# A hybrid of scan, attention and STU on one core: a convolution half in thirds, first products ahead of the scans, longer attention tails, tables of the last STU fetched earlier

## The chip, the core and the metric

The kernel runs on one core of a Trainium2 chip. The metric is the device time of one execution in microseconds, the median of several. The engines are TensorE (PE, its weight loads PEld), VectorE (DVE), ScalarE (ACT), GpSimd (POOL) and SyncE (SP), which here issues nearly all DMAs. Each engine works through its own instruction list in order; semaphores tie them together.

## The reference, cut to what matters

Input x has shape (4, 48, 48, 128), so 4 images of L = 2304 tokens with 128 channels, all in float32.

```python
# layer 0
xz = x_groupnormed @ in_proj_w.T             # 2 * 256 channels: xin, z
xc = silu(depthwise_conv3x3(xin) + conv_b)   # 256 channels = two halves of 128
xs = four orders of xc (rows, columns, both reversed)
dt = softplus(dt_proj(x_proj(xs)))
h  = h * exp(dt * A) + dt * xs * B           # 4 scans, 16 states, 2304 steps
y  = sum of the scans, layernorm, * silu(z)
x  = x + y @ out_proj_w.T
# layer 1
t  = x + softmax(n(x) n(x)^T) n(x)           # n: layernorm over channels
t  = t + STU(n(t))                           # 16 causal convolutions along the tokens, each projected
```

## The kernel before, in words

**Stages.** The images go through a pipeline of stages, one after the other in time. The opening (`prologue`) normalises an image, projects it and computes the convolution. The scans of an image run over 24 chunks (4 orders, 6 chunks of 384 tokens), each with 8 units of 4 scans. Then an epilogue and the attention of that image follow; the next image's `prologue` and the first steps of its scans are woven into the attention. The STU of an image runs on TensorE beside the scans of the next image; beside image 0's scans a mixture of weights is computed instead. The last image's STU (`stu3`) has no scans to run beside, and comes alone at the end.

**Opening.** `taps(h)` computes the 3x3 convolution of channel half h on VectorE, by 9 instructions over the whole image (128x2304): one at L276, eight at L278. `silu(h)` follows in three thirds: tanh on ScalarE (L287), the product on VectorE (L291). The padded input `xpad` stands in a pool called `turn`. For image 0, `run` issues all of the prologue, then `begun` runs through `begin_scans`, whose steps prepare the first chunks: a projection of `xc` on TensorE (L412), copied to `xd` (L419); a second projection (L429) copied to `dt` (L432); softplus (L443); `dx` = dt times xc (L465); both stored to DRAM (L454) and loaded back replicated over partitions as `rep` (L459); rows of `xd` are loaded as `bc` (L485). `start_y` then sets up the sums `ya` (L325). Chunks in row order take 8 image rows each.

**Scans.** A `Ring` of 4 or 5 buffers in PSUM holds the decays. Its constructor zeroes two columns of each buffer on VectorE (L341). `scans` first spreads two `bc` rows into ring buffers (L500), enters two units (L508, on VectorE, or on POOL for three of the eight) and computes decays with exp (L517). Then, for each unit, it issues four scans (L524), and between them `more(share)` takes so many steps of the generator `work` (STU or mixture) as the share of its columns asks. The first step of `conv` in the STU uses tables `tt`, of which the first are loaded in the attention; ScalarE copies results between its products (L1208, L1212, L1215, L1216), issued some columns late (`later`, `do_late`).

**Attention.** `attention` runs over five pieces of queries with 18 key tiles each: 90 slots. A slot issues a product s (L852), its exp (L854), and the value product of three slots before (L844). When a piece is done, its `tail` advances by one step in each slot: the sum is copied from PSUM (oT, L1043), transposed on TensorE (otr, L1047), divided by its denominator and added to T (L1050 to L1058), stored (L1060), loaded back in another token order (L1066), normalised (statistics L1072 to L1078, the result u on ScalarE at L1082), half sums taken (L1084), transposed (utr, L1088), copied and stored. For the last image a tail ends after L1060. In each slot pieces of the next prologue, sorted by cost, are woven in.

**The last STU.** `stu3` loads for each item (block, filter) five tables (L1422) and a weight tile G (L1425), two items ahead; at a block's start inputs `ux`, the mixed weights `mue` and the residual (L1431 to L1436). Per item there are five products (L1446), copies and sums, and a projection (L1480) one item later. `finish3` prepares the inputs of later blocks beside it; its load `fx` is L1361, its statistics L1365.

What sets the order: the lists are written out by the generators above, in program order, with no planner. All DMAs of one engine's queue are issued in order, and a DMA first waits until an earlier one on its semaphore, eight issues back, has landed.

Of the kernel before, what the change touches and what calls it, by code (L numbers as in the profile page):

```python
# [8 lines left out]
F32 = mybir.dt.float32  # L9
# [51 lines left out]
def hybrid_kernel(ctx: ExitStack, tc: tile.TileContext, a: dict, out: bass.AP):  # L61
# [118 lines left out]
    def prologue(b, pool, mm_tile):  # L180
# [87 lines left out]
        def nothing():  # L268
            pass

        def taps(h):
            def tap(t):
                dy, dx = divmod(t, 3)
                x = xpad[:, dy:dy + H, dx:dx + W]
                if t == 0:
                    nc.vector.tensor_scalar(xc[h], x, cw[:, h, 0:1], cb[:, h:h + 1], ALU.mult, ALU.add)  # L276
                else:
                    nc.vector.scalar_tensor_tensor(xc[h], x, cw[:, h, t:t + 1], xc[h], ALU.mult, ALU.add)  # L278
            return [(nothing, Slow(lambda t=t: tap(t), 2.65), t == 0) for t in range(9)]

        def silu(h):
# [30 lines left out]
        for i in range(n):  # L312
            proj(1, i, 0)
            if i % 2:
                tasks.append(zs_[9 + i // 2])
                tasks.append(silu(0)[i // 2])
        tasks.extend(taps(1))
        tasks.extend(silu(1))
        return tasks

    def start_y(b):

# [12 lines left out]
    class Ring:  # L335


        def __init__(self, pool, n, name):
            self.t = [pool.tile([P, 512], F32, tag=f"ring{i}", name=f"{name}_{i}") for i in range(n)]
            for t in self.t:  # L340
                nc.vector.memset(t[:, 0:CS + 2:CS + 1], 0.0)  # L341
            self.free = list(range(n))

        def take(self):
# [263 lines left out]
    def scans(b, chunks, preps, front, sp, back, ring, finish, work, work_cols):  # L608

        units = [Unit(ch, h, q) for ch in chunks for h, q in quads]  # L610
        total = len(chunks) * CHUNK_COLS + work_cols
        done = [0]

        def more(share):

            while done[0] < share * total:
                cols = next(work, None)
                if cols is None:
                    break
                done[0] += cols  # L620

        def enter(s):

            if s + 2 < len(units) and units[s + 2].pool:
                units[s + 2].enter(sp.s, ring)
            if 0 <= s + 1 < len(units) and not units[s + 1].pool:
                units[s + 1].enter(sp.s, ring)

        wanted, issued = [], [0]

        def fill(left=0):

            while wanted and ring.free:
                wanted.pop(0).spread(ring)
            while len(ring.free) > left and issued[0] < G4 * len(units):
                i = issued[0]
                issued[0] += 1
                units[i // G4].decay(i % G4, ring)

        def scan(s, g):  # L640
            fill()
            units[s].scan(g, ring)

        def spread(s):
            if s < len(units) and not units[s].pool:
                wanted.append(units[s])

        def prepare(s):

            ci, j = divmod(s, len(quads))  # L650
            for c in range(ci + 1, ci + 5):
                if c < len(chunks) and 0 <= s - len(quads) * c + LEAD[c % 2] < STEPS[c % 2]:
                    done[0] += next(preps[c]) or 0

        def refill(s, i):

            if 0 <= s < len(units) and s // len(quads) + 1 < len(chunks):
                u, nxt = units[s], chunks[s // len(quads) + 1]
                if u.h == NH - 1:
                    nxt.fetch(i + u.q, front)  # L660

        pending = []
        spread(0)
        fill(len(ring.free) - 1)
        enter(-2)
        enter(-1)
        spread(1)
        fill(1)
        for s in range(len(units) + 2):
            real = s < len(units)  # L670
            enter(s)
            prepare(s)
            if real:
                scan(s, 0)
            more((s + 0.25) / len(units))
            next(finish, None)
            if 1 <= s <= len(units):
                units[s - 1].times_c(s >= len(units) - (units[0].ch.b == 0))
            if real:
                scan(s, 1)  # L680
            if pending:
                pending.pop().add_y()
            prepare(s)
            more((s + 0.5) / len(units))
            next(finish, None)
            spread(s + 2)
            if real:
                scan(s, 2)
            more((s + 0.75) / len(units))
            next(finish, None)  # L690
            prepare(s)
            if real:
                scan(s, 3)
            refill(s - 2, Q4)
            refill(s + 1, 0)
            if s >= 2:
                units[s - 2].sum_c(back.psy)
                done[0] += CS
                if units[s - 2].q == Q4 - 1:
                    pending.append(units[s - 2])  # L700
            more((s + 1) / len(units))
            next(finish, None)
        for u in pending:
            u.add_y()
        for _ in work:
            pass
# [330 lines left out]
    def tail(b, J, T, po, pool, ps, last):  # L1037
# [4 lines left out]
        oT = pool.two.tile([P, 512], F32, tag="oT", name=f"oT{b}_{J}")  # L1042
        nc.vector.tensor_copy(oT[:, :P * n], po[:, :P * n])  # L1043
        yield
        p = ps.trs.tile([P, 4, C], F32, tag="tr", name=f"otr{b}_{J}")[:, :n]
        for j in range(n):
            nc.tensor.transpose(p[:, j], oT[:, j * P:(j + 1) * P], ident)  # L1047
# [34 lines left out]
            nc.scalar.activation(u[:k, J, j], x[:k, j], AF.Identity, bias=mv[:k, j, 3:4], scale=mv[:k, j, 2:3])  # L1082
        yield
        nc.vector.tensor_tensor(sums[:k, J], u[:k, J, 0:2], u[:k, J, 2:4], ALU.add)  # L1084
        yield
        p = ps.trs.tile([P, 512], F32, tag="tr", name=f"utr{b}_{J}")[:, :4 * k]
        for j in range(4):
# [305 lines left out]
            yield  # L1393
        nc.sync.dma_start(ud3[:, :, 1 + P * G:1 + P * (G + 1)], x)

    def stu3(b, pool, ps, u3, ue):

# [7 lines left out]
        tts, Gs, S, U, now = {}, {}, {}, {}, {}  # L1407
        last = pool.one.tile([P, KF], F32, tag="last", name="last3")
        nc.vector.memset(last, 0.0)
        PT = (3, 1, 4, 0, 2)  # L1410
        Y = 3 * (P + 1)

        def fetch(n):
            if n >= len(items):
                return
            bl, k = items[n]
            hi = P * (bl + 1)
            for pt in PT:
                t = tts[n, pt] = pool.tt.tile([P, 2 * L3], F32, tag="tt", name=f"t3{n}_{pt}")[:, :2 * hi].rearrange(
                    "p (e i) -> p e i", e=2)  # L1420
                row = fd3[k, pt, 0]
                nc.sync.dma_start(t, bass.AP(row.tensor, row.offset + L3 - hi, [[1, P], [L3 + P, 2], [1, hi]]))  # L1422
            parts = PARTS3[bl]
            Gs[n] = pool.tt3.tile([P, 2, 3, C], F32, tag="G", name=f"G3{n}")
            nc.sync.dma_start(Gs[n][:, :, :len(parts)], gd[k, :, :, parts[0][2]:parts[-1][2] + 1])  # L1425

        def begin(bl):
            parts = PARTS3[bl]
            lo, hi = P * bl, P * (bl + 1)
            now["x"] = pool.one.tile([P, 8, P], F32, tag="ux", name=f"ux3{bl}")  # L1430
            nc.sync.dma_start(now["x"][:, 2:], ud3[:, :, 1 + lo:1 + hi])  # L1431
            nc.sync.dma_start(now["x"][:, :2], ud3[:, 4:, lo:hi])
            now["mu"] = pool.one.tile([P, 3, 3, C], F32, tag="mue", name=f"mue3{bl}")
            nc.sync.dma_start(now["mu"][:, :len(parts)], mud[:, parts[0][2]:parts[-1][2] + 1])
            now["T", bl] = pool.two.tile([P, 6, C], F32, tag="res", name=f"res3{bl}")
            nc.sync.dma_start(now["T", bl], td[6 * lo:6 * hi].rearrange("(p j) c -> p j c", j=6))  # L1436

# [122 lines left out]
        for _ in other:  # L1560
            pass

    def begun(pieces):

        for x in pieces:
            pass
        return x

    def stu_alone(b, env):
        work = stu(b, env, 1)  # L1570
        next(work)
# [5 lines left out]
        pool.close()  # L1577
        tabs.close()

    turn = Stage(tc, "p", "left", one=(1, SB))  # L1580
    begin0 = Stage(tc, "pp", "right", mm=(4, PSUM))
    once = Stage(tc, "once", "right", one=(1, SB))
    bank["mm"] = begin0.mm, ("t",)
    run(prologue(0, turn.one, mm_tile), 3, weights(once.one))
    turn.close()
    once.close()
    front = Stage(tc, "f0", "left", one=(1, SB), xd=(2, SB), rep=(3, SB))
    first = begun(begin_scans(0, front))
    begin0.close()
    start_y(0)  # L1590
    for b in range(B):
# [13 lines left out]
        turn = Stage(tc, f"t{b}", "left", one=(1, SB))  # L1605
        if b + 1 < B:
            tabs = Stage(tc, f"k{b}", "right", four=(4, SB))
        back = Stage(tc, f"a{b}", "right", one=(1, SB), two=(2, SB), five=(5, SB))
        xn = back.one.tile([P, NT, C], F32, tag="xn", name=f"xn{b}")
        xnT = back.one.tile([P, L], F32, tag="xnT", name=f"xnT{b}")  # L1610
# [31 lines left out]
        for i in range(slots - BEGIN):  # L1642
            next(at)
            if not more:
                next(made, None)
            while parts and (spent < share * (i + 1) or i == slots - BEGIN - 1):
                spent += costs.pop(0)
                parts.pop(0)()
        if more:
            turn.close()  # L1650
            front = Stage(tc, f"f{b + 1}", "left", one=(1, SB), xd=(2, SB), rep=(3, SB))
# [17 lines left out]
    ps = Stage(tc, "endp", "right", psa=(1, PSUM), psc=(2, PSUM), psi=(1, PSUM), psp=(1, PSUM))  # L1669
    bank["mm"] = ps.psa, ("mm",)  # L1670
    ended = (x for G in range(1, N3) for x in finish3(G, extra, u3, ue))
    for i, _ in enumerate(stu3(B - 1, pool, ps, u3, ue)):
        next(ended, None)
    ps.close()
    pool.close()
    extra.close()


# [57 lines left out]
```

## Time and profile before

| | us |
|---|---|
| median of 3 runs | 5449.74 |
| lowest, highest | 5448.53, 5450.31 |
| the profiled execution | 5450.86 |
| its span in the profile | 5448.9 |
| PE busy | 4753.7 (87%) |
| DVE busy | 4320.4 (79%) |
| ACT busy | 3213.1 (59%) |
| POOL busy | 3646.6 (67%) |

Roughly, in the span: opening of image 0 until 117, its scans until 1060, epilogue and attention until 1299; then scans and STU from 1299 to 2260, 2497 to 3460 and 3690 to 4660, with attentions between; the last STU from 4843 on. Shares over the whole span mix these stages, so each stage has to be read by itself. A timeline line gives the start, the busy time, the engine, the source line, the operation with its output and inputs, its shape and its number; in brackets stands the idle time of the engine ahead of it, and what ended it. `SPq` are DMA issues.

### The profile page before, as it was taken

How to read it: one execution, taken by the hardware profiler on the slowest of the kernel's cores; microseconds unless marked ns; L12 is line 12 of the kernel's file. 1: busy time of each engine (PE TensorE's matmuls, PEld its weight loads, DVE VectorE, ACT ScalarE, POOL GpSimd, SP SyncE). 2: the span in 40 equal slices, each digit the busy share in tenths (PEclk: the TensorE clock that was granted, in tenths of full speed). 3: DMA queues.
4: the chain of work that ended last, by engine and by line, in shares of the span. 5: the costliest groups of instructions: out<-in, count | busy, mean ns of one | idle time of the engine just before them, and what ended most of it. 6: DMA issues, size and time to landing. Idle time of an engine off the chain costs nothing. (4 is left out here: it accounts for less than half of the span.)

```text
span 5448.9 us, 71245 instructions
## 1 busy us (share of the span) xinstructions
PE 4753.7 (87%) x23372; PEld 3059.5 (56%) x23372; DVE 4320.4 (79%) x5308; ACT 3213.1 (59%) x6829; POOL 3646.6 (67%) x1881
## 2 busy tenths in 40 slices
PE   4656655698999999998999999898999999989999
PEld 1211211255666666645666666545666666559987
DVE  7999999856999999856999999658999999423211
ACT  3666666546777767456777766457777666432111
POOL 1999998713989999605999999407999999201100
PEclk7777777799999999999999999999999999999999
DMA  4445545404887777416777787227877786136543
GB/s 123 157 156 171 171 153 165 128 27 143 248 257 254 251 258 253 134 34 193 239 259 254 242 269 252 84 75 208 252 246 260 249 262 230 37 83 153 151 142 91
DMA packets 732184, 996.11 MB, mean 183 GB/s; under 512 B 108968, under 2 KB 580648, under 8 KB 731752
## 3 DMA queue, kind: packets, MB, share of 16 engines
q1 hardware_dynamic: 725992, 988.26, 57.6%
q10 hardware_dynamic: 5824, 3.30, 0.3%
q8 instruction: 187, 3.06, 0.2%
q14 instruction: 181, 1.48, 0.1%
HBM read 873.03 MB, written 118.31 MB: 182 GB/s over the span
## 5 line engine op out<-in xcount | busy, mean ns | idle before, releaser
L524 DVE TENSOR_TENSOR_SCAN s<-ring,s 128x385 f32<-128x385 f32 x3072 | 2691.5, 935 | 88.8 <-ACT ring L517 88.0
L534 POOL TENSOR_TENSOR s<-s,bc 128x1536 f32<-128x1536 f32 x763 | 2423.4, 3179 | 95.2 <-DVE s L524 39.0
L517 ACT ACTIVATE ring<-rep,A 128x384 f32<-128x384 f32 x3072 | 1760.2, 584 | 873.9 <-DVE s L508 537.2
L508 POOL TENSOR_TENSOR s<-rep,bc 128x1536 f32<-128x1536 f32 x288 | 994.7, 3454 | 152.4 <-DMA rep<-dtdud 81.2
L542 PE MATMUL y<-s,csum 128*32 128x384 f32 x6144 | 712.5, 538 | 184.0 <-POOL s L534 130.5
L508 DVE TENSOR_TENSOR s<-rep,ring 128x1536 f32<-128x1536 f32 x480 | 829.6, 1729 | 40.5 <-issue 19.9
L1192 PE MATMUL cx<-tt,u 128*128 128x252 f32 (+7 forms) x2880 | 621.9, 357 | 89.9 <-ACT cy L1208 88.9
L1192 PEld LDWEIGHTS cx<-tt,u 128*128 128x128 f32 x2880 | 501.7, 192 | 306.6 <-ACT cy L1208 135.4
L1192 PE MATMUL cx<-tt,us 128*128 128x252 f32 (+7 forms) x2880 | 617.3, 356 | 36.0 <-ACT U L1216 34.2
L1192 PEld LDWEIGHTS cx<-tt,us 128*128 128x128 f32 x2880 | 496.4, 193 | 196.7 <-issue 70.9
L1192 PE MATMUL cy<-tt,u 128*128 128x252 f32 (+5 forms) x2880 | 603.9, 351 | 0.0
L1192 PEld LDWEIGHTS cy<-tt,u 128*128 128x128 f32 x2880 | 490.7, 191 | 150.3 <-issue 99.4
L1258 PE MATMUL pr<-U,G 128*128 128x288 f32 (+4 forms) x1344 | 435.5, 451 | 6.8 <-DMA G<-gd 6.8
L1515 POOL TENSOR_TENSOR t<-s,s 128x512 f32<-128x512 f32 x48 | 63.4, 1320 | 521.7 <-ACT s L1513 521.7
L542 PEld LDWEIGHTS y<-s,csum 128*32 128x32 f32 x6144 | 126.0, 112 | 503.0 <-issue 237.8
L972 PE MATMUL G<-M,W 128*128 128x256 f32 (+3 forms) x512 | 242.3, 590 | 178.8 <-ACT Gm L948 81.2
L854 ACT ACTIVATE e<-s,shift 128x512 f32<-128x512 f32 (+1 forms) x360 | 230.7, 643 | 275.6 <-PE s L852 275.6
L852 PE MATMUL s<-xnT 128*128 128x512 f32 (+1 forms) x720 | 339.8, 557 | 12.9 <-ACT xnT L812 12.9
L844 PE MATMUL o<-e,xn 128*128 128x512 f32 (+1 forms) x720 | 335.4, 550 | 0.0
L1258 PEld LDWEIGHTS pr<-U,G 128*128 128x128 f32 x1344 | 232.4, 192 | 147.0 <-issue 89.2
L972 PEld LDWEIGHTS G<-M,W 128*128 128x128 f32 x512 | 106.9, 242 | 319.3 <-issue 111.3
L532 POOL COPY carry<-s 128x4 f32<-128x4 f32 x640 | 121.3, 189 | 230.8 <-DVE s L524 228.7
(236 smaller groups left out, 5029.5 us busy)
## 6 DMA issues: line engine op xcount, KB each, us to landing
rep<-dtdud SPq DMA_DIRECT2D x768, 384.0 KB
bc<-xdd SPq DMA_DIRECT2D x768, 192.0 KB
tt<-fd SPq DMA_DIRECT2D x144, 577.0 KB
tt<-fd SPq DMA_DIRECT2D x144, 451.0 KB
tt<-fd SPq DMA_DIRECT2D x144, 325.0 KB
dtdud<-dt SPq DMA_DIRECT2D x192, 192.0 KB
dtdud<-dx SPq DMA_DIRECT2D x192, 192.0 KB
t<-fd SPq DMA_DIRECT2D x80, 384.0 KB
```

The source lines that it names most:

```text
L508: eng.tensor_tensor(s, self.ch.rep[self.h][:, :, 1], bt.unsqueeze(1).to_broadcast([P, G4, CS]), ALU.mult)
L517: nc.scalar.activation(ring.body(self.dA[g]), ch.rep[self.h][:, g, 0], AF.Exp, scale=A[:, ch.k, self.h * G4 + g, self.q:self.q + 1])
L524: nc.vector.tensor_tensor_scan(s, ring.decays(i, ch.rev), s, 0.0, ALU.mult, ALU.add)
L532: nc.gpsimd.tensor_copy(carry[:, self.h, self.q].unsqueeze(2), self.s[:, :, end:end + 1])
L534: eng.tensor_tensor(self.s, self.s, ch.bc[Q4 + self.q].unsqueeze(1).to_broadcast([P, G4, CS]), ALU.mult)
L542: nc.tensor.matmul(ch.y[g * DL:(g + 1) * DL, :CS], csum, self.s[:, g], start=(self.q == 0), stop=(self.q == Q4 - 1))
L844: nc.tensor.matmul(po[J][:, :w], xn[:, i], e[:, :w], start=(i == 0), stop=(i == NT - 1))
L852: nc.tensor.matmul(p[:, :w], xnT[:, i * P:(i + 1) * P], xnT[:, 512 * J:512 * J + w], start=True, stop=True)
L854: nc.scalar.activation(e[:, :w], p[:, :w], AF.Exp, bias=shift)
L972: nc.tensor.matmul(p[:, :n], W[:, q if t else 0, i], M[t][:, i].unsqueeze(1).to_broadcast([P, n, C]), start=(t == 0 and i == 0), stop=(t = ...
L1192: nc.tensor.matmul(p4[:, 1:3, v - (hi - at):] if g else p4[:, 0:4:3, v - (hi - at):], x, t[:, :, hi - 1 - at + J * P:end if end >= 0 else ...
L1258: nc.tensor.matmul(o if q else o.rearrange("p f r m -> p r f m"), G, U[n][:, 4 * q:4 * q + 4, v0:v1].rearrange("p (a b) m -> p a b m", a=2 ...
```

## The change

Six edits.

1. `taps` takes a range of image rows. For image 0 only, half 1 of the convolution is computed by thirds of 16 rows (128x768). The first third, its tanh and product stay in the prologue. The tasks of the other two thirds go to a list `late`, from which each step of `begin_scans` takes two (the first six steps) or one. `turn`, with `xpad`, is closed after that, and has moved to the other side of SBUF. `begun` is gone.
2. The ring's zeroing moves from VectorE to ScalarE, as copies of zeros.
3. In `scans` of images 1 to 3 three steps of the STU are taken ahead of the loop over units.
4. A tail has one more step after the copy of oT, and two more between the half sums and the transposes of u.
5. For the last STU the five tables of item 0 and the first `mue` are loaded into a pool `pre` of their own, during image 3's attention. Loading is put into two functions, `table3` and `mixed3`; other items load as before.
6. The later `mue` tiles use that pool too.

In the changed kernel's instruction lists the order on TensorE is the same but for the transposes of the tails; on POOL it is unchanged.

```diff
-        def taps(h):
+        def taps(h, lo=0, hi=H):
             def tap(t):
                 dy, dx = divmod(t, 3)
-                x = xpad[:, dy:dy + H, dx:dx + W]
+                x, o = xpad[:, dy + lo:dy + hi, dx:dx + W], xc[h][:, lo:hi]
...
-        tasks.extend(taps(1))
-        tasks.extend(silu(1))
+        if b:
+            tasks.extend(taps(1))
+            tasks.extend(silu(1))
+            return tasks
+        third, gates = H // 3, silu(1)
+        late[:] = [f for i in range(1, 3) for t in (*taps(1, i * third, (i + 1) * third), gates[i]) for f in t[:2]
+                   if f is not nothing]
+        tasks.extend(taps(1, 0, third))
+        tasks.append(gates[0])
         return tasks
...
-                nc.vector.memset(t[:, 0:CS + 2:CS + 1], 0.0)
+                nc.scalar.copy(t[:, 0:CS + 2:CS + 1], none[:, :2])
...
         fill(1)
+        for i in range(3 if units[0].ch.b else 0):
+            done[0] += next(work)
         for s in range(len(units) + 2):
...
         nc.vector.tensor_copy(oT[:, :P * n], po[:, :P * n])
         yield
+        yield
         p = ps.trs.tile([P, 4, C], F32, tag="tr", name=f"otr{b}_{J}")[:, :n]
...
         nc.vector.tensor_tensor(sums[:k, J], u[:k, J, 0:2], u[:k, J, 2:4], ALU.add)
+        yield
+        yield
         yield
...
+    def table3(pool, tag, k, pt, hi, name):
+
+        t = pool.tile([P, 2 * (L3 if tag == "tt" else P)], F32, tag=tag, name=name)[:, :2 * hi].rearrange(
+            "p (e i) -> p e i", e=2)
+        row = fd3[k, pt, 0]
+        nc.sync.dma_start(t, bass.AP(row.tensor, row.offset + L3 - hi, [[1, P], [L3 + P, 2], [1, hi]]))
+        return t
+
+    def mixed3(pool, bl):
+
+        parts = PARTS3[bl]
+        t = pool.tile([P, 3, 3, C], F32, tag="mue", name=f"mue3{bl}")
+        nc.sync.dma_start(t[:, :len(parts)], mud[:, parts[0][2]:parts[-1][2] + 1])
+        return t
...
+        tts.update({(0, pt): t for pt, t in zip(PT3, ready)})
...
-            for pt in PT:
-                t = tts[n, pt] = pool.tt.tile([P, 2 * L3], F32, tag="tt", name=f"t3{n}_{pt}")[:, :2 * hi].rearrange(
+            for pt in PT3 if n else ():
+                tts[n, pt] = table3(pool.tt, "tt", k, pt, hi, f"t3{n}_{pt}")
...
+            now["mu"] = mixed3(pre.one, bl) if bl else ready[5]
...
-    turn = Stage(tc, "p", "left", one=(1, SB))
+    turn = Stage(tc, "p", "right", one=(1, SB))
...
-    first = begun(begin_scans(0, front))
+    for i, first in enumerate(begin_scans(0, front)):
+        for f in range(2 if i < 6 else 1):
+            if late:
+                late.pop(0)()
+    assert not late
+    turn.close()
...
+        else:
+            pre = Stage(tc, "pre", "right", one=(1, SB))
...
+        if not more:
+            ready = [table3(pre.one, f"t{pt}", 0, pt, P, f"t3{pt}") for pt in PT3] + [mixed3(pre.one, 0)]
```

## The prediction

> **What bounds the kernel now.** I read busy time in 100 us stretches first, then the waits by engine, then the timeline at the four places the change touches. Columns after the stretch: PE, weight loads, DVE, ACT, POOL (us and instructions), granted clock, DMA share, GB/s.
>
> ```profile
> 200.00:300.00 100.00, 61.32 (x249) 20.40 (x250) 97.93 (x102) 67.32 (x148) 94.76 (x49) 0.78 0.52 169
> 1200.00:1300.00 100.00, 97.09 (x254) 45.30 (x252) 46.93 (x90) 51.98 (x88) 5.79 (x7) 1.00 0.25 84
> 3200.00:3300.00 100.00, 99.16 (x532) 66.70 (x534) 98.67 (x106) 68.72 (x147) 92.66 (x44) 1.00 0.77 260
> 5200.00:5300.00 100.00, 100.00 (x450) 83.61 (x449) 17.67 (x38) 10.83 (x19) 7.60 (x6) 1.00 0.46 140
> ```
>
> Image 0's scans are DVE's, attention is PE's, scans beside the STU fill DVE and PE together (DVE ends last: at 2261 the epilogue waits for scan results while the STU ended at 2252), the last STU is PE's. So whatever starts a stage sooner is kept to the end, since stages follow one another. The change works at the seams.
>
> **A. Opening, image 0.** Before:
>
> ```profile
> 69.57 21.20 DVE L278 SCALAR_TENSOR_TENSOR xc<-xpad,cw,xc 128x2304 f32<-128x2304 f32 x8
> 90.86 1.58 ACT L287 ACTIVATE th<-xc 128x768 f32<-128x768 f32 x2 [24.17 <-DVE xc L278]
> 92.75 4.21 PE L412 MATMUL xp<-xc,xw 128*128 128x384 f32 x6 [26.20 <-DVE xc L291]
> 101.90 1.58 ACT L443 ACTIVATE dt<-dt 128x768 f32<-128x768 f32 x2
> 105.30 2.55 SPq L459 DMA_DIRECT2D rep<-dtdud  x4
> 114.42 3.44 POOL L508 TENSOR_TENSOR s<-rep,bc 128x1536 f32<-128x1536 f32 x1 [81.25 <-DMA rep<-dtdud]
> 117.81 3.50 DVE L524 TENSOR_TENSOR_SCAN s<-ring,s 128x385 f32<-128x385 f32 x4
> ```
>
> PE idles 26.2 us for the whole conv of half 1, though the first chunks read a third of it. Price of a third: L291 is the tap's operation at 768 columns, 0.958 us, against 2.614 at 2304; so a fixed 0.13 us per instruction, and 0.04 between two. Eight taps 7.95, the first (1.47 at full width) 0.55: 8.5 us a third, 25.5 for three, 2.8 more DVE than now. After: taps 68.06 to 76.6, tanh and gate (0.97 + 0.96, as at 91.74) to 78.5, PE starts there, 14.2 sooner. In ACT's order the second third's tanh stands between the dt copies, and waits for DVE: 78.5 + 8.5 = 87.0. Behind it wait two dt copies, the table load (1.28) and softplus: softplus at 90.2 instead of 101.9, **11.7** sooner, dx at 91.4, rep's load issued at 93.9, landing 103.0 if it takes the 9.1 us it takes now. Meanwhile DVE, in its new order: second gate to 88.9, two taps to 91.4, dx to 92.4, the rest of the third to 98.4, gate to 100.3, chunk 1's dx to 101.3, two ya (2.74) to **104.1**. That is later than rep, so DVE sets the start: L508 at 104.2 instead of 114.48, **10.3 us gained**. ACT loads tanh's tables in the hole before 98.4 and needs no load for exp, which now follows tanh; five ring zeroings (some 0.2 us each, like the 128x4 copy) fit before 103. If DVE loses its cover here the loss is one for one; bounds 7 and 11.4 (the dx gain).
>
> Here a rule speaks against the change: the Trainium skill, "VectorE: DVE Perf Modes", "The DRAIN you can't avoid", says that after each operation the next waits for roughly its duration less 266 ns. By it a 768-column tap occupies 1.65 us, 27 instructions some 43 us, and L508 starts near 122, 7 us later than now. But by the same rule the full taps would come every 4.96 us; the row above shows eight in 21.20, 2.65 each. I take the row.
>
> **B. Attention tails, three images.** The longer tails:
>
> ```profile
> 1172.74 0.86 DVE L1072 BATCH_NORM_STATS2 ust<-tu 128x6 f32<-128x128 f32 x4
> 1174.17 1.01 POOL L1077 TENSOR_TENSOR umv<-umv,mhalf 128x4 f32<-128x4 f32 x1 [24.58 <-DVE umv L1076]
> 1175.50 1.65 ACT L1082 ACTIVATE u<-tu,umv 128x128 f32<-128x128 f32 x4 [5.72 <-POOL umv L1078]
> 1176.05 1.63 PE L1088 MATMUL utr<-ident,u 128*128 128x128 f32 x4 [4.62 <-ACT u L1082]
> ```
>
> PE stops at 1171.4 for u, since DVE reaches the statistics late behind conv taps of 2.61. DVE's list ahead of the statistics holds the same work after the change (taps and T updates swap), so u still ends at 1177.15. PE now passes ip, S, o, S, o (2.4 us) first and stops for an ip bank and for exp: one more exp stands before u, but the next stands behind it, so S of step 17 starts at 1177.6 instead of 1181.71, with 0.45 of transposes to come: 3.6 gained. Then DVE, whose idle 3.39 us for z behind u goes, brings oT at 1187.7 instead of 1190.3, and otr's wait of 1.38 falls.
>
> The page "TensorE: Matmul & The Clock Gate" (What's actually happening) halves the clock after an idle window of about 3.4 us; the two waits left (0.9 and 2.3) would escape it and I would have 4.1. The trace has four S at 1115 taking 5.40 instead of 3.44 after only 1.80 idle. With that cold stretch PE arrives at otr later, oT is ready, and 3.3 stay. I take **3.5, three times: 10.5**; bounds 0 (wait merely moved) and 5.5 an image. The tails of the other pieces show no such wait, the last tail of an image runs without slots between its steps and keeps its 0.8. A tail now takes 18 steps, and a piece has 18 slots, so the next tail isn't held up.
>
> **C. Scan start, three images.**
>
> ```profile
> 1299.42 3.42 DVE L508 TENSOR_TENSOR s<-rep,ring 128x1536 f32<-128x1536 f32 x2 [0.52 <-ACT ring L500]
> 1303.80 1.34 PE L1192 MATMUL cx<-tt,u 128*128 128x144 f32 x4 [5.92 <-ACT cy L1208]
> 1309.73 3.51 DVE L524 TENSOR_TENSOR_SCAN s<-ring,s 128x385 f32<-128x385 f32 x4 [0.96 <-ACT ring L517]
> ```
>
> Zeroing on ACT, idle 6.54 us there, takes DVE's 0.09 and 0.52 away. The three early steps issue prime, the first products, ux, mue, G and a table load, in the same order on PE and SP as before; only ACT's cy copy moves, past one decay that waits for DVE. PE goes on at 1298.3, later held by a ring slot, some 4 ahead; ACT's idle 1.26 for PE at 1307.5, and DVE's 0.96, go. **1.6 each, 4.8.** The next DVE waits (1.49 for POOL, 1.76 and 3.73 around ACT and its table loads) have other causes: bounds 0.5 and 4.
>
> **D. Last STU.**
>
> ```profile
> 4842.89 2.60 SPq L1422 DMA_DIRECT2D t<-fd  x5
> 4846.98 2.07 PE L1446 MATMUL x<-t,ue 128*128 128x256 f32 x4 [6.82 <-DMA t<-fd]
> 4860.43 0.33 SPq L1361 DMA_DIRECT2D fx<-td  x1
> 4867.81 1.26 DVE L1365 BATCH_NORM_STATS2 fs<-fx 128x6 f32<-128x128 f32 x6 [14.51 <-DMA fx<-td]
> 4871.16 6.27 PE L1480 MATMUL p<-U,G 128*128 128x144 f32 x30 [6.12 <-DVE U L1537]
> ```
>
> Five tables and mue (six loads) move ahead of image 3's fx load and of two stores on SP; fx is needed 20 us after its issue, so they hide. PE starts at 4840.2, 6.8 sooner. But U stands behind fx on DVE, and fx on SP behind the second ux (mue's lane before). With six loads fewer in front (2.60 + 0.46 issue, 1.25 MB, at 311 GB/s some 4 us) fx goes at about 4856, lands at 4863.4, p starts at 4866.8: **4.4**, bounds 2 and 6.8.
>
> **Sum**: 10.3 + 10.5 + 4.8 + 4.4 = 30.0. The profiled execution took 5450.86 (span 5448.9 and 1.96 around it), 1.1 over the median of 5449.74; so 5420.9 by it, **5420** by the median.
>
> **Rivals.**
> - Tails only move PE's wait (the stop for exp behind u speaks for it, the freed DVE against): without 10.5, 5430.
> - The opening is held by DMA: the rep load or chunk 1's stores queue behind the same transfers as now and A is 4 (two waits on landed loads before 114 speak for it; nothing new is put in the queue): 5426.
> - PE's lead in C removes the waits of 1.76 and half of 3.73 too: 3.6 more an image, 5409.
> - Slower: ACT's cy copy now stands ahead of the third decay, and waits for PE. Should cx come late (its table or u not there), every decay and scan waits behind it. cx ends at 1297.9, the decay is possible at 1302.3: 4.4 us of cover. It decides from 14 us late in each image (4.4 and a third of 30); at 20 it is +16, 5466 by the median. The table was loaded in attention, which speaks against.
>
> **Chances**: forecast 0.57 (own range 5413 to 5427), tails 0.17, DMA 0.09, lead 0.15, slower 0.02. Range 5407 to 5433. No change is within 10.9 us, 0.2%, about what measurement can tell: All cases but the last stay faster; a little of the tails case falls to no change should A fail with it: 0.95, 0.03, 0.02.
>
> **What would show it.** PE's first L412 wait near 12 us and the first scan at 107.5; utr without a wait and an S wait near 2 to 3; no 5.9 wait for cy; PE's wait for t gone, p's U wait ending near 4867 on a common shift. Wrong if DVE's idle in the scans rises by 10 us an image, or rep lands after 110.

## The result, and the profile after

The changed kernel takes 5427.35 us (median of 6 runs, 5424.71 to 5433.06) against 5449.00 (6 runs, 5447.10 to 5450.31) for the kernel before. The ratio is 0.9963, with a 95% interval of 0.9951 to 0.9975 that lies clear of 1: about 20 us less (21.7 by the medians). The profiled execution took 5428.15 with a span of 5425.8, so 23.1 of span were gained there. The forecast was 5420, with a range of 5407 to 5433.

In what follows a **mark** is the start of one instruction in the trace, and its shift is how much sooner it comes than in the trace of before. Where the shift grows, time is gained; where it shrinks, time is given back. Line numbers are those of the kernel shown; from the edit of the conv on, the changed kernel's are 9 to 27 higher than before's.

The opening, rows of the timeline of the changed kernel (start, duration, engine, line, operation; in brackets the idle time before it and what ended it):

```profile
68.57 8.40 DVE L278 SCALAR_TENSOR_TENSOR xc<-xpad,cw,xc 128x768 f32<-128x768 f32 x8
78.95 4.21 PE L421 MATMUL xp<-xc,xw 128*128 128x384 f32 x6 [12.60 <-DVE xc L291]
87.95 0.84 ACT L287 ACTIVATE th<-xc 128x768 f32<-128x768 f32 x1 [2.45 <-DVE xc L278]
90.85 1.58 ACT L452 ACTIVATE dt<-dt 128x768 f32<-128x768 f32 x2
94.91 2.55 SPq L468 DMA_DIRECT2D rep<-dtdud  x4
102.33 2.74 DVE L334 TENSOR_SCALAR ya<-xc,dsum 128x2304 f32<-128x2304 f32 x2
104.03 4.34 POOL L517 TENSOR_TENSOR s<-rep,bc 128x1536 f32<-128x1536 f32 x1 [71.12 <-DMA rep<-dtdud]
104.99 3.41 DVE L517 TENSOR_TENSOR s<-rep,ring 128x1536 f32<-128x1536 f32 x2
108.32 3.50 DVE L533 TENSOR_TENSOR_SCAN s<-ring,s 128x385 f32<-128x385 f32 x4
```

TensorE's wait is 12.6 instead of 26.2, softplus comes at 90.85, and VectorE goes from the second ya straight into its first product. The first scan starts 9.5 us sooner.

The same view at the tail of the first piece in image 0's attention, where before TensorE stood 4.62 us ahead of utr:

```profile
1163.87 2.61 DVE L278 SCALAR_TENSOR_TENSOR xc<-xpad,cw,xc 128x2304 f32<-128x2304 f32 x1
1164.01 0.91 PE L254 MATMUL ip<-xT,win 128*128 128x384 f32 x2 [0.87 <-DVE z L261]
1164.60 1.94 POOL L1090 TENSOR_TENSOR umv<-umv 128x4 f32<-128x4 f32 x1
1166.58 1.65 ACT L1094 ACTIVATE u<-tu,umv 128x128 f32<-128x128 f32 x4 [6.59 <-POOL umv L1090]
1168.13 0.45 ACT L865 ACTIVATE e<-s,shift 128x256 f32<-128x256 f32 x1
1168.63 1.22 PE L863 MATMUL s<-xnT 128*128 128x256 f32 x2 [3.72 <-ACT e L865]
1170.50 1.06 PE L1102 MATMUL utr<-ident,u 128*128 128x128 f32 x4
1171.36 1.82 PE L863 MATMUL s<-xnT 128*128 128x512 f32 x2
1175.39 1.02 PE L863 MATMUL s<-xnT 128*128 128x512 f32 x2
1181.40 0.38 PE L1059 MATMUL otr<-ident,oT 128*128 128x128 f32 x2
```

utr has no wait. But TensorE stands 0.87 for z and then 3.72 for an exp that is queued behind u on ScalarE: 4.6 us as before, a few products further on. The products behind the stop are slow in both kernels: the granted clock was 0.50 from 1168.60 to 1171.36 and 1.00 again from 1173.45 on, and behind the stop of before it was 0.59 from 1176.05 to 1178.74. And u itself is late: GpSimd's second product, 4 columns wide, takes 1.94 us, where it took 0.20 before.

The scan start of image 1, and the last STU:

```profile
1286.78 3.41 DVE L517 TENSOR_TENSOR s<-rep,ring 128x1536 f32<-128x1536 f32 x2
1290.11 3.50 DVE L533 TENSOR_TENSOR_SCAN s<-ring,s 128x385 f32<-128x385 f32 x4
1292.86 1.34 PE L1206 MATMUL cx<-tt,us 128*128 128x144 f32 x4 [2.07 <-ACT U L1230]
...
4821.52 1.03 PE L1473 MATMUL x<-t,ue 128*128 128x256 f32 x4
4829.20 2.08 PE L1473 MATMUL x<-t,ue 128*128 128x256 f32 x4 [3.20 <-DMA t<-fd]
4836.01 0.60 SPq L1375 DMA_DIRECT2D fx<-td  x1
4843.15 1.26 DVE L1379 BATCH_NORM_STATS2 fs<-fx 128x6 f32<-128x128 f32 x6 [15.98 <-DMA fx<-td]
4846.51 6.56 PE L1507 MATMUL p<-U,G 128*128 128x144 f32 x30 [6.34 <-DVE U L1564]
```

At the scan start VectorE has no wait ahead of the product or of the scans. In the last STU the first products start without a wait, the second item's tables now end one of 3.20, and U still ends 6.34 us, since VectorE stands behind fx as before.

The shifts, added up over the stages, for this profile and for a second one of the same kernel (taken among the experiments):

| part | forecast | first profile | second profile |
|---|---|---|---|
| A, to the end of image 0's scans | 10.3 | 10.5 | 8.5 |
| B, first to last oT of three attentions | 10.5 | 1.4 + 1.4 + 1.8 = 4.6 | 1.3 + 1.5 + 1.4 = 4.2 |
| C, last oT to first scan, three images | 4.8 with the next row | 3 x 0.7 = 2.1 | 3 x 0.7 = 2.1 |
| C, the scans of images 1 to 3 | | 0.8 + 3.9 - 1.1 = 3.6 | 1.1 + 2.4 + 0.9 = 4.4 |
| end of scans to first oT, four epilogues | 0 | -2.4 | 1.0 |
| D, last oT to the end | 4.4 | 4.6 | 7.5 |

The columns add up to the 23.1 us of span gained in the first profile and, to a tenth, the 27.8 in the second. Both are measured from one trace of before, whose execution (5450.86 us) lies above all medians of that kernel (5445 to 5449). A came out as worked out in the first profile (the second lost a race that is told of below), and B brought less than half. For D one pair of profiles says little, since the last stage varies: it takes 600.0 to 605.5 us (mean 603.6) in the eight profiles that have the changed kernel's code there, and 606.4 to 610.1 (mean 607.9) in the three with the code of before. By the means D is 4.3 us, which is what the forecast had. The scans vary as much, so that their 3.6 lies near the forecast is in part luck.

### The profile page after: what moved, and what is told of

Same layout as the page of the kernel before. It is cut to its first block, busy times and chain, and to the rows that moved or that the text cites. A ratio compares the mean times of both kernels' runs of the same rounds, so it can differ in the third digit from the quotient of the medians.

```text
span 5425.8 us, 71249 instructions
## 1 busy us (share of the span) xinstructions
PE 4748.4 (88%) x23372; PEld 3052.8 (56%) x23372; DVE 4326.5 (80%) x5309; ACT 3213.5 (59%) x6846; POOL 3657.3 (67%) x1881
```

## The experiments

Twelve more runs were made (the last is the changed kernel again), in three groups, each beside runs of the kernel before on the same chip; those had medians of 5447.96 (48 runs), 5445.01 (13) and 5446.64 us (29). The marks of all, as gains over the trace of before, except that the last stage is given by its length:

| kernel | first scan | tails, images 0, 1, 2 | seams | scans 1, 2, 3 | last stage | ratio [95%] |
|---|---|---|---|---|---|---|
| before | 0 | 0 | 0 | 0 | 610.1 | 1 |
| changed | 9.5 | 1.4, 1.4, 1.8 | 0.7 | 0.8, 3.9, -1.1 | 605.5 | 0.9963 [0.9951, 0.9975] |
| open_only | 8.3 | 0.0, -0.1, -0.1 | 0.1 | -0.6, 2.6, -0.2 | 606.4 | 0.9985 [0.9979, 0.9992] |
| no_tails | 9.1 | 0.1, -0.1, -0.1 | 0.7 | -1.9, 2.3, -2.8 | 604.3 | 0.9975 [0.9967, 0.9982] |
| u_later | 10.2 | 6.4, 6.2, 6.2 | 0.7 | -0.6, 0.8, -0.1 | 605.5 | 0.9939 [0.9927, 0.9952] |
| no_steps | 8.9 | 1.8, 1.7, 1.7 | 0.7 | -2.9, -1.1, -2.7 | 605.0 | 0.9977 [0.9970, 0.9984] |
| no_tables | 6.7 | 1.3, 1.7, 1.7 | 0.7 | 0.8, 4.2, 1.0 | 607.2 | 0.9969 [0.9958, 0.9980] |
| fx_early | 9.7 | 1.3, 1.7, 1.5 | 0.7 | 0.8, 4.3, 0.9 | 595.9 | 0.9944 [0.9931, 0.9956] |
| best | 7.0 | 6.3, 6.2, 6.2 | 0.8 | -0.4, 2.9, 1.4 | 598.5 | 0.9932 [0.9919, 0.9944] |
| dve_zero | 8.7 | 1.4, 0.7, 1.7 | 0.0 | -0.4, 4.1, -0.2 | 600.0 | 0.9968 [0.9957, 0.9980] |
| best_ya | 11.1 | 6.4, 6.2, 6.2 | 0.7 | -0.8, 1.0, -0.2 | 595.9 | 0.9921 [0.9907, 0.9934] |
| no_c | 5.4 | 1.4, 1.7, 0.9 | 0.0 | -1.6, -0.5, -2.8 | 604.6 | 0.9982 [0.9975, 0.9988] |
| ot_only | 5.8 | 0.7, 0.5, 0.6 | 0.8 | -3.2, -0.1, -0.8 | 601.3 | 0.9974 [0.9964, 0.9983] |
| after_again | 7.2 | 1.3, 1.5, 1.4 | 0.7 | 1.1, 2.4, 0.9 | 602.6 | 0.9963 [0.9950, 0.9975] |

The seams repeat within 0.1 and the tails mostly within 0.5, so one profile decides there. The first scan, the scan stages and the last stage vary by 3 us and more between kernels that share their code; there the times decide, or nothing does.

### The opening alone (open_only)

The kernel before with the first edit only:

```diff
-        tasks.extend(taps(1))
-        tasks.extend(silu(1))
+        if b:
+            tasks.extend(taps(1))
+            tasks.extend(silu(1))
+            return tasks
+        third, gates = H // 3, silu(1)
+        late[:] = [f for i in range(1, 3) for t in (*taps(1, i * third, (i + 1) * third), gates[i]) for f in t[:2]
+                   if f is not nothing]
+        tasks.extend(taps(1, 0, third))
+        tasks.append(gates[0])
```

> The kernel before with the opening by thirds alone. Theory (the marks of the changed trace carry over: the opening keeps what it gains to the end): the first scan and the end of image 0's scans come 9.5 to 10.5 us sooner than before, and so does the end: 5439 us. Rival (the opening only moves work that image 0's scans, full on DVE, take back, and the shift of 10.5 comes from the zeroing on ScalarE): under 7 us, 5442 or more.

Measured: 0.9985, that is 8.2 us less (4.4 to 11.4). The first scan comes 8.3 us sooner, the end of image 0's scans 9.4, a little less than expected. The shift stays between 6 and 11 up to the last STU, as far as the scans' and epilogues' own variation lets one see; at the end of this profile it is 14.5, since the last stage took 606.4 us and not 610.1 with the same code. What the opening gains is kept. VectorE zeroes the ring here, so the marks also refute the rival that the zeroing makes the shift; the time alone could not tell 9.5 from under 7.

### The tails: what the steps are worth (no_tails, ot_only)

no_tails takes out all three steps; ot_only only the last two of this diff, and leaves the one after oT:

```diff
         nc.vector.tensor_copy(oT[:, :P * n], po[:, :P * n])
         yield
-        yield
...
         nc.vector.tensor_tensor(sums[:k, J], u[:k, J, 0:2], u[:k, J, 2:4], ALU.add)
-        yield
-        yield
         yield
```

> The changed kernel without the three added steps in the tails. Theory (the stop only moved: TensorE no longer waits 4.6 us for u at utr, but 0.9 for z and 3.7 for an exp that stands behind u on ScalarE, and both pay a cold clock after it; what the steps bring is otr's wait of 1.4 and its seam): 1.5 to 1.8 us an image are lost, 4.5 to 5.5 in all: 5432. Rival (the steps are worth the 3.5 an image of the forecast, and something else in the attention took 2 us an image): 10.5 slower, 5438.

> The changed kernel with the step after oT alone; the two steps ahead of u's transposes are taken out. Theory (those two steps only move the stop of 4.6 us from utr to the exp behind u; the step after oT is what brings the 1.4 to 1.8 an image): the attention's marks gain 1.4 to 1.8 an image as in the changed kernel, and the time is the same, 5427. Rival (the two steps bring it and the step after oT nothing): 5 more, 5432.

Measured in no_tails: the gain in the tails falls from 1.4 to 1.8 to nothing (0.1, -0.1, -0.1). So the three steps are worth 1.5 us an image, as the theory had it, not 3.5. The time is 0.9975 against 0.9963: 6.5 us, with intervals that overlap, too wide to choose between 5 and 10 alone.

In ot_only the gain is 0.7, 0.5 and 0.6, less than half of the 1.4 to 1.8 that the theory expected. TensorE's stop is back at utr:

```profile
1168.85 1.63 PE L1100 MATMUL utr<-ident,u 128*128 128x128 f32 x4 [4.86 <-ACT u L1094]
```

otr has no wait there either, but the stop is 0.24 us longer than the 4.62 of before, and four groups of products behind it are slow (S 1.06, o 1.06, ip 1.49, S 0.99 us) where before three were (ip 1.49, S 1.06, o 0.76). So this part of the theory was wrong: the step after oT brings 0.6 an image, and the two others the remaining 0.9, though the stop that they were to remove only moved. The time, 0.9974 (0.9964 to 0.9983), is too wide to add anything.

### u later on ScalarE (u_later)

The two steps ahead of utr go, and four are put ahead of u's activations in the tail of the first piece, so that four more exps stand in front of them in ScalarE's order:

```diff
+        for i in range(6 if J == 0 else 2):
+            yield
-        yield
-        yield
         for j in range(4):
             nc.scalar.activation(u[:k, J, j], x[:k, j], AF.Identity, bias=mv[:k, j, 3:4], scale=mv[:k, j, 2:3])
...
         nc.vector.tensor_tensor(sums[:k, J], u[:k, J, 0:2], u[:k, J, 2:4], ALU.add)
-        yield
-        yield
         yield
```

> The changed kernel with the two added steps ahead of the transposes taken out, and four steps put ahead of u's activations in the tail of the first piece. Theory (ScalarE's order is the cause: u waits there for GpSimd's mean and rstd, and the exps that TensorE needs stand behind it): with u behind four more exps both stops of 4.6 us and the cold clock after them go, 5 to 6.5 us an image, 15 to 20 in all: 5409. Rival (VectorE's late statistics and z set the pace there, so TensorE stops for z or an ip bank instead): at most 2 us an image, 5422 to 5428.

Measured: 0.9939, 5412.59 us, and 6.4, 6.2 and 6.2 us in the tails. The timeline at the same place:

```profile
1162.81 0.91 PE L254 MATMUL ip<-xT,win 128*128 128x384 f32 x2 [0.87 <-DVE z L261]
1163.41 1.94 POOL L1090 TENSOR_TENSOR umv<-umv 128x4 f32<-128x4 f32 x1
1165.88 1.64 ACT L1094 ACTIVATE u<-tu,umv 128x128 f32<-128x128 f32 x4
1167.01 0.89 PE L1100 MATMUL utr<-ident,u 128*128 128x128 f32 x4
```

GpSimd is as late as before, u ends as late after it, but nothing waits for it: ScalarE goes from an exp into u without idling. TensorE's stops are the 0.87 for z and, 12 us later, one of 0.36 for another z, and the S and o behind the first take 0.59 as they do ahead of it. That settles the cause: the order on ScalarE, not VectorE's late statistics. The difference between 6.3 and 1.5 also shows what such a stop costs, some 4.8 us of waiting and slow clock.

### The scan start (no_steps, dve_zero, no_c)

no_steps takes out the early steps (the first two lines of this diff), dve_zero zeroes the ring with VectorE again (the other two), no_c does both:

```diff
-        for i in range(3 if units[0].ch.b else 0):
-            done[0] += next(work)
...
-                nc.scalar.copy(t[:, 0:CS + 2:CS + 1], none[:, :2])
+                nc.vector.memset(t[:, 0:CS + 2:CS + 1], 0.0)
```

> The changed kernel without the three early steps of the STU at each scan start. Theory (they are worth the waits that they removed: VectorE's 0.96 for a decay, and some of TensorE's 5.9 for cy): 1 us an image is lost, 3 in all: 5430. Rival (TensorE's lead is lost again within the scans, which VectorE sets): no change, 5427 within 1.5. Second rival (the lead carries further into the stage: the gains of 0.9 and 3.9 in the scans of images 1 and 2): 5 or more are lost, 5432 up.

> The changed kernel with the ring's slots zeroed by VectorE again, not by ScalarE. Theory (0.09 of work and 0.52 of waiting ahead of the first product at each scan start come back, as the marks show it, where the first product is 0.6 to 0.7 us further ahead in every image; in the opening nothing waits for it): 1.8 us in all, 5429. Rival (VectorE's lead there is taken back by ScalarE's decay, which the early steps hold): no change, 5427.

> The changed kernel with the scan start as before: the ring's slots zeroed by VectorE and no early steps. Theory (the two belong together; zeroing on ScalarE brings 0.65 an image ahead of the first product and the steps some 0.8 in the scans, 4 to 5 in all): 5431 to 5432. Rival (without the early steps the zeroing on ScalarE costs time in the scans, where the kernel with it alone lost 6.7 us in three images, so that leaving out both costs less than leaving out the steps alone): the scans' marks fall by 2 us an image less than there. Second rival (C brings nothing): 5427.

The zeroing is clear from the marks: with VectorE's memset the seam gains nothing (0.0), with ScalarE's copy 0.7 in every image of every kernel. That is 2.1 us in all; the time says 2.7 (0.9968 against 0.9963), with intervals that overlap by far.

The steps seem to be worth more than expected: 0.9977 against 0.9963, 7.6 us with intervals that overlap a little, where the theory said 3. Leaving out both costs 10.4 (0.9982), with intervals that just meet. The rival of no_c, that zeroing on ScalarE costs time without the steps, is not borne out: the scans are as slow with VectorE's zeroing (-1.6, -0.5, -2.8) as without (-2.9, -1.1, -2.7). By the marks the ten profiles with the steps gain 2.1 us in their three scan stages together (from -4.1 to 6.0), the four without, before among them, lose 2.5 (from -6.7 to 1.8). So the steps bring some 4.6 by the means of the marks and 7.6 by the times, and neither is sharp. The lead that TensorE gets does seem to carry into the scans, as one of the rivals of the prediction had it. The wait that shrinks is VectorE's for decays: from the first scan of a stage to its last, summed over the three stages, it is 70.7 to 76.3 us (mean 72.5) with the steps and 73.4 to 78.6 (mean 76.3) without, 3.8 of the 4.6. Why a few products issued early shorten waits all along a stage stays open.

### The last STU (no_tables, fx_early)

no_tables loads the first tables and mue inside the stage again (the first two lines of this diff and what hangs on them). fx_early takes the first step of the finishing work, fx's load, ahead of the stage's loads (the added line):

```diff
-        if not more:
-            ready = [table3(pre.one, f"t{pt}", 0, pt, P, f"t3{pt}") for pt in PT3] + [mixed3(pre.one, 0)]
...
+    next(ended)
     for i, _ in enumerate(stu3(B - 1, pool, ps, u3, ue, pre, ready)):
         next(ended, None)
```

> The changed kernel with the last STU's first five tables and mue loaded inside that stage again. Theory (what the early loads bring is TensorE's wait for the first table, 6.8 to 3.2, and for mue, 2.7 to 1.2, while its wait for U of 6.3 behind the fx load stays): the last stage is 4 to 5 us longer than in the changed kernel, 5432. Rival (the stage's length varies by as much without a change, 605.7 to 609.4 us from the last oT to the end in two kernels that share its code, and the early loads bring nothing): 5427 to 5428, and the waits for table and mue only change places with that for U.

> The changed kernel with the first fx load of the last STU issued one step ahead of that stage's other loads. Theory (U stands behind the statistics of fx on VectorE, and fx stands behind fourteen loads on SyncE's queue): fx lands some 12 us sooner, TensorE's wait of 6.3 for U falls to 2 or less, 4 to 5 us are gained, 5423. Rival (U waits for ScalarE's squares and TensorE's y product anyway): under 1.5 us, 5426.

no_tables: TensorE's waits in the stage's start are 6.8 for the table, 2.2 for mue and 5.3 for U, near the 6.8, 2.7 and 6.1 of before; the stage takes 607.2, 1.7 more than in the changed kernel's first profile and 3.6 more than the mean of the eight with its code, and the time is 3.3 more (0.9969, with intervals that overlap). TensorE's waits in the stage for table, mue or ux, U and s sum to 20.2 us before, 19.3 here and 15.9 in the changed kernel, so by them the early loads are worth 3.4 to 4.3. The rival, that they bring nothing, does not hold.

fx_early gained more than the 4 to 5 us that were expected: 595.9 us against 605.5 in the stage, and 0.9944 against 0.9963 in the time, 10 us. With the stage's variation averaged out it is less: the three profiles with the early fx have a mean of 596.8, the eight without of 603.6, so 6.8.

```profile
4817.15 0.46 SPq L1375 DMA_DIRECT2D fx<-td  x1
4829.25 4.41 PE L1491 MATMUL p<-ux,mue 128*128 128x144 f32 x36
4833.50 3.60 PE L1507 MATMUL p<-U,G 128*128 128x144 f32 x30
```

fx goes ahead of the stage's other loads, and U is there when TensorE wants it. The expectation had left out what the stop does to the clock: the thirty products take 3.60, not 6.56. So the 6.34 of waiting carried 3.0 more behind it. The waits for the second item's table (from 3.20 to 4.47) and for s (from 2.25 to 3.15) grew.

### Both, and the race in the opening (best, best_ya, after_again)

best is u_later with fx_early. best_ya also puts the first of the two products that start ya between the last third's tanh and its gate:

```diff
+    tanh3 = late[-2]
+    late[-2] = lambda: (tanh3(), start_y(0, (0,)))
     for i, first in enumerate(begin_scans(0, front)):
...
-    start_y(0)
+    start_y(0, (1,))
```

> The changed kernel with both: u's activations of the first piece's tail four steps later and the two steps ahead of the transposes taken out, and the first fx load one step ahead of the last STU's other loads. Theory (the two stops are in different stages, so the gains add): 15 to 20 from the first and 4 to 5 from the second: 5408. Rival (the second brings nothing): 5412.5 as u's change alone.

> The kernel with both (u's activations later, first fx load sooner), and of the two products that start ya in the opening the first is put between the last third's tanh and gate, where VectorE stands 0.9 us. Theory (the opening has a race: where GpSimd's first product starts before the second ya, that ya takes 4.58 instead of 1.41 us and the first scan comes at 110.8 to 111.1, not 107.6 to 109.5): the second ya now starts near 101.9, ahead of GpSimd at 102.9 to 103.5, and takes 1.4; the first scan comes at 106.6 to 107.5, and the end 1 to 4 us sooner than the kernel with both, 5405. Rival (the first product of VectorE waits for its own rep load, which lands after GpSimd's): no sooner than 108.5, 5408.

> The changed kernel itself once more, for a second profile and its times on the chip of its variants. Both theories expect 22 us less than the kernel before; the marks at the stages' seams within 0.7 us of the first profile, but for the opening (first scan at 107.6 to 109.5, or at 111 where the second ya loses its race), the scans (within 3 us an image) and the last stage (within 4 us, by how long TensorE's clock stays low after a stop).

best came at 0.9932, 5408.30 us: less than both gains together would give by the times (13 and 10 below the changed kernel; it is 17 below), and more than either. By the marks the gains do add, 14 in the tails and 7 in the last stage. That the 5408 of the expectation was hit is in part luck: the second gain had been put at 4 to 5. The profile of best has a worse opening, with the first scan 2.5 us later than in the changed kernel. The second profile of the changed kernel has the same thing:

```profile
101.43 5.90 DVE L334 TENSOR_SCALAR ya<-xc,dsum 128x2304 f32<-128x2304 f32 x2
102.17 3.95 POOL L517 TENSOR_TENSOR s<-rep,bc 128x1536 f32<-128x1536 f32 x1 [69.58 <-DMA rep<-dtdud]
107.25 3.41 DVE L517 TENSOR_TENSOR s<-rep,ring 128x1536 f32<-128x1536 f32 x2
```

rep landed sooner here, at 102.17 and not 104.03, and that made the opening slower: GpSimd's product started before the second ya, and this ya then took 4.57 us where it takes 1.41 otherwise. In the first profile the ya was there first, and GpSimd's product took 4.34 instead of some 3.5. Of the twelve profiles of this opening, five lost the race (first scan at 110.6 to 112.4) and seven won it (107.6 to 109.5). best_ya removes it:

```profile
102.05 1.41 DVE L335 TENSOR_SCALAR ya<-xc,dsum 128x2304 f32<-128x2304 f32 x1
103.22 3.54 POOL L518 TENSOR_TENSOR s<-rep,bc 128x1536 f32<-128x1536 f32 x1 [70.64 <-DMA rep<-dtdud]
103.38 3.41 DVE L518 TENSOR_TENSOR s<-rep,ring 128x1536 f32<-128x1536 f32 x2
106.71 3.50 DVE L534 TENSOR_TENSOR_SCAN s<-ring,s 128x385 f32<-128x385 f32 x4
```

The first scan comes at 106.71, the earliest of all (in this one profile), and the kernel takes 5401.87 us, 0.9921 (0.9907 to 0.9934): 43 us less than before, and faster than the changed kernel. Its margin over best lies within the intervals; the rows of the opening are what carries it.

## Why the prediction was right, and where it was not

**What bounds it, and that seams are kept**: right. A shift gained in one stage is found at the end of the next, within the few us by which scans and epilogues vary.

**A**: right, to 0.8 us. The third costs 9.1 instead of the 8.5 of the sum (8.40 for eight taps, where 7.95 was said, and 0.67 for the first, where 0.55), softplus came 0.65 later, and so did the first product, at 104.99 against 104.2. That the taps follow one another without a gap was right, 1.05 us from one to the next; the rule of a wait after each operation was rightly set aside. (The section that the prediction cites for it also says that a next operation which is not held starts earlier; whether the taps are such is not shown here.) What the step didn't see is the race at its end. It had VectorE as the last to arrive and took an earlier landing of rep for harmless; in the second profile rep landed 1.9 us sooner, and VectorE's first product started 2.3 us later. The bounds of 7 and 11.4 held for the profiles that won the race, the losers lie at 5.4 to 7.2.

**B**: wrong in size, 1.5 an image instead of 3.5, and this is most of what the forecast missed. The step that failed is "3.3 stay". These are the rows of before that it is measured against:

```profile
1175.26 0.20 POOL L1078 TENSOR_TENSOR umv<-umv 128x4 f32<-128x4 f32 x1
1181.71 0.59 PE L852 MATMUL s<-xnT 128*128 128x256 f32 x2
1185.79 1.02 PE L852 MATMUL s<-xnT 128*128 128x512 f32 x2
1190.34 0.44 PE L1047 MATMUL otr<-ident,oT 128*128 128x128 f32 x2 [1.38 <-DVE oT L1043]
```

Two terms of the sum were mis-sized. First, S of step 17 was to start 4.1 us ahead of the common shift (the 10.45 us that were gained before the attention), and started 2.6 ahead (1168.63 against 1181.71, less 10.45): GpSimd's second product took 1.94 us instead of 0.20, where the sum had said that u ends where it ended. Second, the slow stretch behind the stop, for which the sum let 4.1 fall to 3.3, cost 2.2: S starts its o 1.02 us after itself and not 0.43, o and the transposes behind it take 0.85 and 0.86 and not some 0.43, the 512-column S takes 1.66 and not 0.86 from start to start. The example that the prediction had quoted, four S in 5.40 us instead of 3.44, already had 2.0 in it. With 0.4 for the transposes, as said, nothing is left at 1175.39, which against 1185.79 is a shift of 10.40. What is gained comes after it, where otr no longer waits 1.38 for oT. Even that has another reason than the one given: oT was to come 2.6 us ahead of the common shift and comes 0.3 ahead (it ends at 1179.53 against 1190.29), but otr now stands one step later. The prediction had looked at before's stop as 4.62 of waiting and at its successor as something smaller. Both are the same stop with the same slow clock after it. The rival "the wait only moves" was right about the mechanism, and said no gain at all where 1.5 came.

**C**: the zeroing came out at 0.7 an image, as the 0.09 and 0.52 said. The steps were undersized, as far as the scans' variation lets one say: 4.8 was said for both, 4.6 + 2.1 = 6.7 came by the means of the marks and 10 by the times. The new wait at this place, 2.07 for U, stands where before cy ended one of 5.92, and VectorE's rows beside it show no wait. The slower case, decays queued behind a cy copy that waits for TensorE, did not arise.

**D**: right, and by its steps. PE starts at 4821.52, that is 4840.0 on the clock of before (said: 4840.2); fx is issued at 4854.5 (said: 4856) and p starts at 4865.0 (said: 4866.8). By the end of the thirty products 5.9 are gained; some 2.2 are lost again where x waits 2.25 for s and another thirty products take 5.09 instead of 3.57, and 4.6 is what the whole stage keeps. The load of fx did set the pace of the stage's start, and the change left it behind sixteen others; fx_early shows what was left there.

**The sum**: 30 was said; 20 to 23 came by the times, 23.1 and 27.8 in the two profiles. In the first profile B gave 6 less and C 1 more than said, and the four epilogues, which had been put at nothing, took 2.4. In the second B gave 6 less and the lost race cost 2, while C gave 2 more, the epilogues 1 and D 3. The scans, the epilogues and D differ by as much in kernels that share their code, so B and the lost race are the misses that the runs explain.

## What to carry to other kernels

For a wait on a late value, look at the queue of the engine that makes the value, and not only at the one that reads it. Here two more steps ahead of the transposes that read u moved the stop to the next exp and brought a tail from 0.6 to 1.5 us; four more exps ahead of u on ScalarE removed the stop and brought it to 6.3. Price a stop of TensorE with the slow clock behind it, here 2.2 and 3.0 us on top of stops of 4.6 and 6.3. And where GpSimd and VectorE start work on SBUF at about the same time, ask which is first, and move the one that something waits for ahead, as best_ya does.

## What the runs showed of the hardware that was not expected

**VectorE and GpSimd can block each other for a whole instruction.** The second ya takes 1.41 us alone and 4.57 to 4.62 where GpSimd's product (3.4 to 4.0 us) started first; GpSimd's product takes 4.25 to 4.7 where the ya was first. The Trainium skill says this on the page "SBUF — State Buffer", section "SBUF: two separate sides": the port pair that the two share is an exclusive lock, and of a GpSimd operation and a VectorE operation in a two-port mode or with two SBUF inputs, whichever starts first holds it for its whole instruction. The rows agree. It also fits the product of 4 columns in the tails, which a convolution tap with two SBUF inputs runs beside: 1.94 us, ending at 1166.54 where the tap ends at 1166.48, while at the same place before VectorE was idle and it took 0.20. Over all fourteen traces this product takes 0.19 to 0.21 us in the 101 cases in which VectorE stands still at its start, and 1.76 to 1.95 in the 66 in which a full-width tap runs. Not every pair blocks: VectorE's product of rep with ring, one input of which lies in PSUM, has a median of 1.73 us whether or not one of GpSimd's large products runs beside it. None of these blocked times is shown as a wait; each stands inside the duration of an instruction.

**The slow clock after the same stop lasts differently.** The thirty products behind U's stop, in the changed kernel and in the one with VectorE's zeroing, whose last stage is the same code:

```profile
4846.51 6.56 PE L1507 MATMUL p<-U,G 128*128 128x144 f32 x30 [6.34 <-DVE U L1564]
```

```profile
4845.36 5.47 PE L1507 MATMUL p<-U,G 128*128 128x144 f32 x30 [6.49 <-DVE U L1564]
```

6.56 after 6.34 with a granted clock of 0.54, 5.47 after 6.49 with 0.66, and 3.57 with a clock of 1.00 (at 4858.43 in the changed kernel). At the end of image 1's scans TensorE stands 4.38 us for GpSimd in both kernels, and then the eight mu products take, in the kernel before,

```profile
2258.40 1.43 PE L542 MATMUL y<-s,csum 128*32 128x384 f32 x8 [4.38 <-POOL s L534]
2261.73 5.49 PE L734 MATMUL mu<-ya,dmean 128*128 128x512 f32 x8
```

and in the changed one

```profile
2244.87 1.51 PE L551 MATMUL y<-s,csum 128*32 128x384 f32 x8 [4.38 <-POOL s L543]
2248.19 3.86 PE L745 MATMUL mu<-ya,dmean 128*128 128x512 f32 x8
2257.20 2.63 PE L745 MATMUL mu<-ya,dmean 128*128 128x512 f32 x4 [2.78 <-DVE ya L752]
```

The granted clock was 0.67 over the eight products in the first and 1.00 in the second. The 1.6 us gained were lost again, with more, at the next wait, which was 2.78 instead of 1.51, with a clock of 0.72 behind it (2257.2 to 2259.9). The page "TensorE: Matmul & The Clock Gate", section "What's actually happening", says that the window in which activity is counted runs freely, so that the moment of the change depends on where in it the work falls. The rows agree with that, but no run here holds the window's phase fixed, so it is not shown. What is shown bounds what one profile can say: between profiles with the same code in that stage, the epilogue of image 1 differs by up to 6.6 us and the last stage by up to 5.5.
